# A four-stage transformer block on one core: weighing TensorE's changes of array layout together with the stages' lag

## The chip, the cores and the metric

The kernel runs on one core of a Trainium2 chip. The metric is the time of one execution on the device in microseconds; the median of several runs is compared. Profiles are of one execution each.

## The reference

The input x holds 16 sequences of 512 positions with 256 features, in float32. Four residual steps follow each other; each begins with a layer norm:

```python
x = x + attn_a(layernorm(x))   # 16 heads of 16; window |i-j| <= 32 and 4 global positions; biases
x = x + ffn(layernorm(x))      # silu(x wg') * (x wu'), 768 wide, then wd'; integer weights / 127
x = x + attn_b(layernorm(x))   # 16 heads; causal; rotary q and k in the numerator,
                               # num = exp(q_rot k_rot' / 4), den = sum over all keys of exp(q k' / 4)
x = x + ffn(layernorm(x))      # the same weights as above
```

In `attn_b` the denominator is summed over all 512 keys with the unrotated q and k, and the causal mask is applied to num / den.

## The kernel before

The four steps are four **stages**, named a, f, b and h. Each stage handles one sequence at a time, as 4 tiles of 128 positions (NT) and 2 halves of the features (NC). Up to four sequences are under way at once, since x has 4 buffers; so at any time the stages work on different sequences.

TensorE's work comes in **pieces** of a few matmuls. Each piece has a layout of the array (`lying`):

- FULL: 128 rows and 128 columns. These are the transposes after the layer norm (`lt_*`, L454), the projections (`psc_*`, L534, and `psv_*`, L512), the output products (`po_*`, L488), stage a's transposes of its weights (`tp`, L772, and `pgp`, L809 and L811) and its small global products (`ya` at L855, `sgp`, `gq`, `vgp`, `tg`, `og`, `yg`).
- ROWS: four strips of 32 rows, used at once, each with the products of one head. These are the scores `sa` of stage a (L663, 4 pieces per sequence), and in stage b the scores for the denominators `dn` (L1102, 16 pieces) and for the numerators `nm` (L1162, 10 pieces). Such a piece takes four of the eight PSUM banks.
- COLS: four strips of 32 columns: weights times values, `ya` of stage a (L842, 8 pieces) and `yb` of stage b (L1222, 10 pieces).

The other engines take the results out of PSUM. For `dn`, ScalarE applies the exponential with a sum to each of the four banks (L1083). For `nm`, ScalarE writes exponentials to `ptb` (L1129, two buffers), GpSimd cuts them to the causal part (L1138), and `yb` uses them. For `tp`, ScalarE and VectorE copy to `pt` (three buffers), and `ya` uses those.

The order of the instructions is written by a planner in Python, the class `Plan`, when the program is built. Every stage is a set of generators (threads) that yield one operation after another, each with an engine, an estimated time, what it needs (names with due times) and the buffers that it takes. `Plan.run` keeps a time for each engine and each buffer. At each step it computes when every thread's next operation could start, looks at the earliest, and gathers the operations of that engine that could start within 0.05 us of it (`soon`). On TensorE it chooses among them by a key; first comes a rank (-2 for the transposes after the layer norm, 0 for most). The planner charges BORDER, 0.2 us (L84), when the layout of a piece differs from that of the one before (`self.lying`).

`progress` (L137) says how far a thread's stage is: the number of its sequence, plus the stage's lead (LEAD, L192), plus the TensorE time that this stage has had for this sequence, divided by the stage's SHARE (L193). The thread that is least far is served first.

The planner's order is kept on all engines and on SP's DMA queue, as the instruction streams are emitted in the order of its choices. So another choice on TensorE also moves the operations that follow from it on the other engines.

## Time and profile before

| | before |
|---|---|
| median of 3 runs | 2706.07 us (2703.79 to 2711.95) |
| the profiled execution, its own time | 2707.05 us |
| its span, first to last instruction | 2705.3 us |
| busy: TensorE, VectorE, ScalarE, GpSimd | 2645.4, 1572.2, 1461.4, 740.3 us |
| mean granted clock of TensorE | 0.992 |

The busy time of TensorE (PE) is the time in which at least one matmul was under way. Weight loads have a row of their own (PEld). A group of instructions is named by its line, engine and operation, with the tile that it writes and those that it reads.

### The profile page before, as it was taken

To read this page: it belongs to the slowest core of one execution; us is meant where nothing else is said; L and a number is where in the kernel's file an instruction comes from. 1 tells how busy PE (TensorE), PEld (TensorE's weight loads), DVE (VectorE), ACT (ScalarE), POOL (GpSimd) and SP (SyncE) were. 2 spreads that over 40 slices of the span, in tenths; PEclk is the share of its full clock that TensorE was granted. 3 is DMA by queue.
4 is the path that set the end of the run, shared out by engine and by line. 5 is a ranking of instruction groups with operands and counts; after the bars stand their busy time and mean duration, and the time that the engine had idled before them with its cause. 6 is when DMAs were issued, how large, how long until landed. Compare 5 with 4: busy or idle time off the path is not lost.

```text
span 2705.3 us, 52423 instructions
## 1 busy us (share of the span) xinstructions
PE 2645.4 (98%) x21700; PEld 1511.9 (56%) x21700; DVE 1572.2 (58%) x3062; ACT 1461.4 (54%) x3553; POOL 740.3 (27%) x916
## 2 busy tenths in 40 slices
PE   6999999999999999999999999999999999999997
PEld 4655556455565655656466564655656456564444
DVE  7865656466565655746466564565745557464422
ACT  2346564755547455474645647455474654646472
POOL 4323324032241313313133231322313133130201
PEclk8999999999999999999999999999999999999999
DMA  4000010000000000010000100000000000100000
GB/s 134 24 23 1 5 35 1 23 17 23 17 2 23 17 23 17 1 38 2 23 17 6 34 2 23 17 23 17 2 23 17 23 17 1 31 2 8 1 9 8
DMA packets 26574, 49.10 MB, mean 18 GB/s; under 512 B 2336, under 2 KB 21216, under 8 KB 26336
## 3 DMA queue, kind: packets, MB, share of 16 engines
q1 hardware_dynamic: 24976, 44.83, 5.7%
q8 instruction: 170, 2.79, 0.4%
q10 hardware_dynamic: 1360, 0.93, 0.2%
q14 instruction: 68, 0.56, 0.1%
HBM read 13.77 MB, written 8.39 MB: 8 GB/s over the span
## 4 chain that ended last, share of the span: by engine, by line
PE 90%; DVE 6%; issue 3%; ACT 1%; POOL 1%; DMA 0%; ACTq 0%; POOLq 0%; DVEq 0%
PE dn L1102 10%; PE nm L1162 6%; PE psc_gh L534 6%; PE psc_uh L534 6%; PE po_h L488 6%; PE po_f L488 6%; PE psc_uf L534 6%; PE psc_gf L534 6%; PE yb L1222 5%; PE tp L772 4%; PE sa L663 2%; PE ya L842 2%; PE psv_a L512 2%; PE po_a L488 2%; PE psv_b L512 2%
## 5 line engine op out<-in xcount | busy, mean ns | idle before, releaser
L1083 ACT ACTIVATE dn<-dn 128x512 f32<-128x512 f32 x1024 | 598.1, 584 | 136.7 <-PE dn L1102 135.5
L1129 ACT ACTIVATE ptb<-nm 128x512 f32<-128x512 f32 x640 | 329.7, 603 | 278.3 <-PE nm L1162 278.2
L708 POOL TENSOR_TENSOR sc<-sc,sm 128x1056 f32<-128x1056 f32 x128 | 247.4, 1952 | 227.7 <-DVE sm L706 220.7
L1102 PE MATMUL dn<-kt,qb 32*128 32x512 f32 x2048 | 291.6, 635 | 0.0
L1138 POOL TENSOR_SCALAR_AFFINE_SELECT ptb<-ptb 128x512 f32<-128x512 f32 x256 | 157.9, 636 | 446.2 <-ACT ptb L1129 437.9
L715 ACT ACTIVATE sc<-sc 128x1056 f32<-128x1056 f32 x128 | 138.5, 1096 | 137.4 <-POOL sc L708 136.0
L693 DVE TENSOR_TENSOR sc<-sa,mask 128x512 f32<-128x512 f32 x256 | 159.8, 682 | 59.4 <-PE sa L663 59.1
L534 PE MATMUL psc_gh<-xnt_h,wg_sb 128*128 128x512 f32 x384 | 189.2, 615 | 3.2 <-DVE vb L523 3.0
L1083 ACT ACTIVATION_READ_ACCUMULATOR dn<-dn 128x1 f32 x1024 | 191.7, 187 | 0.0
L1162 PE MATMUL nm<-qr,kr 32*128 32x512 f32 (+3 forms) x2048 | 191.0, 461 | 0.4 <-ACT ptb L1129 0.3
L717 DVE TENSOR_REDUCE sm<-sc 128x8 f32<-128x1056 f32 x128 | 157.3, 1242 | 55.2 <-ACT sc L715 55.2
L534 PE MATMUL psc_uh<-xnt_h,wu_sb 128*128 128x512 f32 x384 | 186.9, 609 | 0.0
L534 PE MATMUL psc_gf<-xnt_f,wg_sb 128*128 128x512 f32 x384 | 182.9, 599 | 1.6 <-DVE xnt_f L462 1.6
L534 PE MATMUL psc_uf<-xnt_f,wu_sb 128*128 128x512 f32 x384 | 183.2, 599 | 0.0
L488 PE MATMUL po_h<-wd_sb,ht_h 128*128 128x256 f32 x768 | 181.3, 386 | 0.0
L1102 PEld LDWEIGHTS dn<-kt,qb 32*128 32x128 f32 x2048 | 90.0, 183 | 160.0 <-ACT dn L1083 88.1
L488 PE MATMUL po_f<-wd_sb,ht_f 128*128 128x256 f32 x768 | 179.2, 383 | 0.0
L1222 PE MATMUL yb<-ptb,vb 128*32 128x512 f32 (+3 forms) x2048 | 170.1, 441 | 8.4 <-POOL ptb L1138 8.3
L421 POOL TENSOR_SCALAR rstd_f<-mv_f 128x4 f32<-128x4 f32 x16 | 3.7, 232 | 613.8 <-DVE mv_f L417 613.8
L488 PEld LDWEIGHTS po_h<-wd_sb,ht_h 128*128 128x128 f32 x768 | 141.0, 190 | 45.9 <-issue 13.3
L706 DVE TENSOR_REDUCE sm<-sc 128x8 f32<-128x1056 f32 x128 | 156.3, 1237 | 0.0
L488 PEld LDWEIGHTS po_f<-wd_sb,ht_f 128*128 128x128 f32 x768 | 141.3, 190 | 26.5 <-issue 3.3
(168 smaller groups left out, 4201.3 us busy)
## 6 DMA issues: line engine op xcount, KB each, us to landing
vw<-va SPq DMA_DIRECT2D x32, 576.0 KB, 5.8
x<-in_x_dram SPq DMA_DIRECT2D x16, 512.0 KB, 3.9
out_dram<-x SPq DMA_DIRECT2D x16, 512.0 KB, 2.9
vw<-va SPq DMA_DIRECT2D x32, 144.0 KB, 5.0
raw_wg_sb<-in_w_gate_dram SPq DMA_DIRECT2D x1, 768.0 KB, 8.8
raw_wu_sb<-in_w_up_dram SPq DMA_DIRECT2D x1, 768.0 KB, 10.2
raw_wd_sb<-in_w_down_dram SPq DMA_DIRECT2D x1, 768.0 KB, 10.9
wqkv_sb<-in_wqkv_dram SPq DMA_DIRECT2D x1, 768.0 KB, 11.7
```

The source lines that it names most:

```text
L488: nc.tensor.matmul(po[:, :D], y_of(c), w_sb[:, c, :], start=(c == 0), stop=(c == n - 1))
L534: nc.tensor.matmul(ps, w_sb[:, kc, lo : lo + P], x_in[:, kc, :], start=(kc == 0), stop=(kc == NC - 1))
L693: nc.vector.tensor_tensor(flat[:, 4 * j : 4 * j + 4, 0:P], ps[j].rearrange("p c two w -> p (c two) w"), mask.unsqueeze(1).to_broadcast([P, ...
L706: nc.vector.tensor_reduce(small[:, 0, hs], part, AX.X, ALU.max, negate=True)
L708: nc.gpsimd.tensor_tensor(part, part, small[:, 0, hs].unsqueeze(2).to_broadcast([P, H // 2, P + NG]), ALU.add,)
L717: nc.vector.tensor_reduce(small[:, 1, hs], part, AX.X, ALU.add)
L1083: nc.scalar.activation(ps[j], ps[j], AF.Exp, scale=SCALE, accum_out=den[:, t, h : h + 1])
L1102: nc.tensor.matmul(ps[j], tiles["qb"][rows, par, oc, t * P : (t + 1) * P], tiles["kt"][rows, oc, :], start=True, stop=True,)
L1129: nc.scalar.activation(pt[:, j, :], ps[j], AF.Exp, scale=SCALE)
L1138: nc.gpsimd.affine_select(out=pt[:, :, at : at + P], in_=pt[:, :, at : at + P], pattern=[[0, 4], [1, P]], compare_op=ALU.is_ge, fill=0.0, ...
L1162: nc.tensor.matmul(ps[j][:, at : at + n], tiles["kr"][rows, oc, c * P : (c + 1) * P], tiles["qr"][rows, par, oc, c * P :], start=True, sto ...
L1222: nc.tensor.matmul(y_ps[rows, c * P :], vb[:, c, 4 * oc + j, par : par + 2, :], pt[:, j, at : at + n], start=len(seen) == 1, stop=len(seen ...
```

## The change

The key by which TensorE's next piece is chosen changes. Before, it had three parts: the rank; then, only if TensorE lies in strips, whether the piece lies otherwise (all changes alike); then the progress. Now it has two: the rank, and the progress plus a price for the change of layout, `turn`, in units of sequences. Staying costs 0. Leaving full products costs 0.15, going from rows to columns or back 1.0, and going from strips to full products 5.0. The leads of the stages f, b and h change also: 1.0, 2.0 and 3.0 become 1.069, 1.854 and 2.806. The rest of the diff is blank lines.

```diff
+    def turn(self, lying):
+
+        if lying == self.lying:
+            return 0.0
+        return TURN["out"] if self.lying == FULL else TURN["in"] if lying == FULL else TURN["mid"]
...
                     key=lambda c: (
                         c[1][4],
-                        self.lying != FULL and c[1][1].lying != self.lying,
-                        self.progress(c[1]),
+                        self.progress(c[1]) + self.turn(c[1][1].lying),
                     ),
...
-LEAD = {"a": 0.0, "f": 1.0, "b": 2.0, "h": 3.0}
+TURN = {"out": 0.15, "mid": 1.0, "in": 5.0}
+LEAD = {"a": 0.0, "f": 1.069, "b": 1.854, "h": 2.806}
 SHARE = {"a": 44.0, "f": 33.0, "b": 66.0, "h": 33.0}
```

## The prediction

> **What bounds the kernel now.** I read the head of the page first, then section 5, then the times by stretch, and last the TensorE instructions in order of time.

> ```profile
> span 2705.3 us, 52423 instructions
> PE 2645.4 (98%) x21700; PEld 1511.9 (56%) x21700; DVE 1572.2 (58%) x3062; ACT 1461.4 (54%) x3553; POOL 740.3 (27%) x916
> ```

> TensorE is busy for 98% of the span and no other engine exceeds 58%. The busy times of six stretches (columns: the stretch, then busy time and instructions of PE, PEld, DVE, ACT, POOL, then TensorE's clock and DMA):

> ```profile
> 0.00:620.00 620.00, 585.66 (x5337) 345.55 (x5338) 397.96 (x761) 312.16 (x726) 195.68 (x244) 0.98 0.10 29
> 620.00:2350.00 1730.00, 1730.00 (x14201) 989.40 (x14200) 1030.00 (x2024) 970.38 (x2386) 475.19 (x583) 1.00 0.06 17
> 2625.00:2706.00 81.00, 62.57 (x386) 32.85 (x384) 17.94 (x37) 25.77 (x50) 12.13 (x19) 0.95 0.04 14
> ```

> From 620 to 2350 us TensorE is busy in every microsecond, and the waits of that stretch name none of TensorE's. The last output product of stage h ends there every 163.6 us, sequence after sequence. So no wait is to be saved in the middle: it changes only if TensorE's own stream gets shorter. The matmuls are the same before and after. What can differ is what lies between them, and that is seen in order of time (columns: start, us until the group's last end, engine, line, names, shape, count; the useful number is the difference of two starts):

> ```profile
> 1210.73 1.98 PE L534 MATMUL psc_gf<-xnt_f,wg_sb 128*128 128x512 f32 x4
> 1212.56 1.88 PE L534 MATMUL psc_uf<-xnt_f,wu_sb 128*128 128x512 f32 x4
> 1214.27 1.88 PE L534 MATMUL psc_gf<-xnt_f,wg_sb 128*128 128x512 f32 x4
> ...
> 1316.59 2.00 PE L1102 MATMUL dn<-kt,qb 32*128 32x512 f32 x16
> 1318.52 1.13 PE L512 MATMUL psv_a<-wv_sb,xnt_a 128*128 128x256 f32 x4
> ...
> 1343.01 1.14 PE L1102 MATMUL dn<-kt,qb 32*128 32x512 f32 x8
> 1344.08 1.98 PE L534 MATMUL psc_uh<-xnt_h,wu_sb 128*128 128x512 f32 x4
> 1346.00 1.14 PE L1102 MATMUL dn<-kt,qb 32*128 32x512 f32 x8
> 1347.07 1.98 PE L534 MATMUL psc_gh<-xnt_h,wg_sb 128*128 128x512 f32 x4
> ```

> A full product between full products takes 1.71 us (1212.56 to 1214.27). Just after row strips it takes 1.83; between row strips on both sides, 1.92 (1344.08 to 1346.00). One dn piece between full products takes 1.07 (1343.01), two in a row 1.93 (1316.59), so the second costs 0.86 and the lone one carries 0.21 extra. Pairing neighbouring pieces over the whole trace gives medians for what entering and leaving add: full products 0.104 and 0.094 us (0.055 to enter where it is a transpose), rows 0.104 and 0.109, columns 0.025 and 0.115. So full to rows costs 0.198, rows to full 0.213, full to columns 0.119, columns to full 0.219, rows to columns 0.134, columns to rows 0.219.

> Counting the changes: 356, 331, 130, 155, 87 and 62 in that order, 1121 in all. At those prices they cost 216 us, 8% of the span; 740 of them, 143 us, lie in 620 to 2350. The end has real idleness instead:

> ```profile
> 2656.83 1.23 PE L1222 MATMUL yb<-ptb,vb 128*32 128x256 f32 x16 [1.94 <-POOL ptb L1138]
> 2666.86 2.20 PE L454 MATMUL lt_h<-ident,xn_h 128*128 128x128 f32 x8 [4.63 <-DVE xn_h L426]
> ```

> From 2625.19 (the last product of h's sequence 14 is out) to 2666.86, stage b of sequence 15 runs alone, and the brackets of this stretch sum to 13.3 us of 41.7, 32% idle.

> [...]

> **The change part by part.** It adds no instruction, DMA, buffer or semaphore by itself; it reorders pieces, and with them the work that follows on ACT, DVE, POOL and SP's queue. No engine but TensorE is over 60% in the middle stretch (DVE 1030 of 1730), so their own cost is nothing while TensorE is behind; without that cover, it would show as brackets like those of the end.

> Step 1, **from strips to the other strips before full products** (1.0 against 5.0; before, both ranked alike). I compared each end of a strip visit in 620 to 2350 with when the pieces run later became ready: columns from the end of their copies on ACT and DVE or of POOL's select, rows from four free banks and their buffers. Of 233 changes from rows to full, a column piece was ready in 32; of 97 from columns to full, a row piece in 10. The other 288 were forced, and the new rule has nothing else to take there.

> Step 2, **full products keep TensorE unless strips are 0.15 behind**. Against stage a's full products b's strips stand as before (0.15 against a lead lowered by 0.146). Stage a's own strips (sa, ya) do change: they no longer win a tie with a's full products and wait for b's next visit. There are 325 visits in 620 to 2350, on average 3.8 us apart; 44 consist of one column piece (33 ya, 11 yb). Attached to a row visit, such a piece saves 0.119 + 0.219 + 0.213 - (0.134 + 0.219) = 0.198 us. The 32 of step 1 are mostly these same pieces. So 44 x 0.198 = 8.7, and the 10 of step 1 another 10 x 0.198 = 2.0: 10.7 us, and over the whole span by changes (1121/740) **16 us**. Bounds: 0, if the pieces still go singly; above, the second rival.

> Step 3, **gathering**. 41 visits are a single nm and 126 a single dn. The dn's I leave: their four exponentials and accumulator reads take 4 x (0.584 + 0.187) = 3.08 us on ACT, and the dn's start 2.99 us apart (1343.01, 1346.00): ACT and the banks set their beat, not the choice. If one nm in four meets another row piece, 10 visits go at 0.198 + 0.213: 4.1 us, over the span **6 us**. Nearest row for the lower bound: none meets, 0.

> Step 4, **the leads**. In the middle they shift phases, which TensorE's full stream hides. In the drain, h comes 0.194 x 163.6 = 32 us earlier, b 24 us earlier, f 11 us later. Between h's sequence 14 and b's 15 this moves 0.048 x 163.6 = 7.9 us of cover away, at 32% idle **2.5 us** lost. Bounds: -5 (b's last chain starts sooner) and +21 (all of h's 32 us uncovered, 10 us, and f's 11 us straight on the end).

> Sum: -16 - 6 + 2.5 = -20 us. The profiled execution took 2707.05 us (span 2705.3), 1.0 above the median of 2706.07; 2707 - 20 = 2687, against the median **2686 us**.

> **The rivals.** *Strips gather strongly.* If full products are held long enough that a quarter of the visits join others, 81 x 0.411 = 33 us in the middle, 50 over the span: 2656 us. For it: visits average only 3.8 us apart, and 211 of 325 hold one piece. Against: 126 of those follow ACT's beat.

> *The order hardly changes what counts.* With 288 of 330 ends forced, and a shift of phases that makes as many single visits as it removes, 3 us are left: 2703 us. The same would show if the lowered lead of b cancelled the 0.15 everywhere.

> *The drain gets longer: slower.* Place: from h14's last product to h15's transposes. Stage b's chain (nm, exponentials, select, yb) doesn't depend on the choice and needs filling work; h14 goes earlier and f15 later, so filling is spent before b15 needs it. Price up to +21 us. It decides once it exceeds what the changes save: with 8 saved instead of 22, the result is 2706 + 21 - 8 = 2719 us. For it: 32% idle there already. Against: b is brought forward too.

> **How the numbers follow.** Forecast 0.53 (2670 to 2698), strong gathering 0.16, no difference 0.13, slower 0.18. A measurement can tell about 0.3%, 8 us, so "same" is 2698 to 2714. Faster is 0.53 + 0.16 = 0.69. The range runs from a little beyond 2656 down to 2648 and up to 2722, past the slower rival; about one in ten lies outside on each side at most.

> **What would show it.** Steps 1 and 2: changes between full products, rows and columns fall from 1121 to about 1010, single ya visits nearly vanish, rows-to-columns and columns-to-rows changes grow above 87 and 62; the prices of each change stay. Step 3: longer nm groups, dn still single at 3 us. Step 4: brackets before yb, dbp and lt_h in the last 100 us sum to 13 to 18 us. The period in the middle falls from 163.6 to about 162.3 us, with no waits of TensorE there. The forecast is wrong if changes don't fall, if TensorE gets waits in the middle, or if the drain loses over 10 us.

## The result, and the profile after

The changed kernel takes 2746.81 us (median of 5 runs, 2745.42 to 2748.78), the kernel before 2706.65 us (5 runs). The ratio is 1.015, with a 95% interval of 1.0137 to 1.0164: slower by 40 us, outside the predicted range. The span of the profiled execution is 2747.0 us, 41.7 us longer.

The head of the page after:

```profile
span 2747.0 us, 52475 instructions
PE 2664.6 (97%) x21700; PEld 1539.5 (56%) x21700; DVE 1556.0 (57%) x3062; ACT 1471.8 (54%) x3553; POOL 739.6 (27%) x916
```

TensorE executes the same 21700 matmuls and stays the bound. But the stretch that had no waits now has some. The waits of TensorE from 620 to 2350 us (engine and piece, who ended the wait; total us, times, longest) and the busy times there (PE, PEld, DVE, ACT, POOL, then clock and DMA):

```profile
PE ya L840 <- DVE pt L775: 26.2, 11, 2.4
```

```profile
620.00:2350.00 1730.00, 1703.80 (x13823) 984.99 (x13827) 1001.30 (x1983) 942.08 (x2273) 471.51 (x578) 0.98 0.06 16
```

It is one wait of 2.38 us in each sequence of this stretch, always the same: `ya`, in the middle of a piece, for a copy to `pt` on VectorE (L775; it was L777 before). All of TensorE's waiting there is this line, 1730.00 - 1703.80 = 26.2 us. Here is one such place, TensorE in order of time (start, us, engine, line, names; in brackets the idle time before):

```profile
984.41 0.66 PE L770 MATMUL tp<-ident,sc 128*128 128x128 f32 x4
984.90 1.96 PE L532 MATMUL psc_qa<-xnt_a,wq_sb 128*128 128x512 f32 x4
986.79 0.43 PE L840 MATMUL ya<-pt,vw 128*32 128x64 f32 x16
989.61 0.56 PE L840 MATMUL ya<-pt,vw 128*32 128x64 f32 x16 [2.38 <-DVE pt L775]
990.10 2.09 PE L1100 MATMUL dn<-kt,qb 32*128 32x512 f32 x8
992.12 1.22 PE L853 MATMUL ya<-pgs,vg 64*128 64x128 f32 x4
993.27 3.62 PE L532 MATMUL psc_uh<-xnt_h,wu_sb 128*128 128x512 f32 x4
```

In the kernel before, the two halves of such a piece (32 matmuls) run as one group:

```profile
1283.84 0.65 PE L842 MATMUL ya<-pt,vw 128*32 128x64 f32 x32
```

In the listing of the changed kernel, look at the lines after the wait, too. The dn piece takes 2.0 us (990.10 to 992.12) where 1.07 is usual, and the up product 3.45 us (993.27 to 996.72) where 1.72 is. The busy times by stretch give the reason (the third column from the end is TensorE's clock):

```profile
974.60:989.60 15.00, 12.62 (x92) 7.00 (x90) 14.69 (x29) 5.85 (x15) 4.92 (x5) 1.00 0.01 2
989.60:996.60 7.00, 6.99 (x32) 3.27 (x33) 1.17 (x3) 2.49 (x8) 0.00 (x0) 0.51 0.00 0
```

After each wait TensorE runs at half clock for 6.83 us, which costs 3.4 us more. And the first of these lines shows VectorE, from which the copy comes, busy for 14.69 of the 15 us up to the end of the wait.

**Where the 41.7 us are.** I counted the changes of layout (1001 instead of 1121) with the prediction's prices, TensorE's idle time before its matmuls, and the stretches at half clock, of which half is lost:

| us | before | after | difference |
|---|---|---|---|
| changes of layout | 215.6 | 192.4 | -23.2 |
| idle time of TensorE | 55.5 | 78.0 | +22.5 |
| lost to half clock (half of 41.8 and 126.3) | 20.9 | 63.2 | +42.3 |
| the rest of the span | 2413.3 | 2413.4 | +0.1 |
| span | 2705.3 | 2747.0 | +41.7 |

The rest is the same within 0.1 us, so for the span as a whole these three terms are enough. The change did save what it was to save; waits took it back, and the clock took nearly twice as much again. By place: stage h's sequence 0 ends 14.9 us earlier, the next twelve sequences (called the middle below) take 44.9 us longer (167.2 us each instead of 163.6), the rest of the span 11.8 us longer. Place by place the three terms leave several microseconds open, because work moves from one stretch to another and because the profile's busy time hides some short waits (dn pairs that take 2.95 us instead of 1.93, below).

### The profile page after: what moved, and what is told of

Its sections match the earlier page's. It is cut to its first block, busy times and chain, and to the rows that moved or that the text cites. A ratio compares the mean times of both kernels' runs of the same rounds, so it can differ in the third digit from the quotient of the medians.

```text
span 2747.0 us, 52475 instructions
## 1 busy us (share of the span) xinstructions
PE 2664.6 (97%) x21700; PEld 1539.5 (56%) x21700; DVE 1556.0 (57%) x3062; ACT 1471.8 (54%) x3553; POOL 739.6 (27%) x916
## 4 chain that ended last, share of the span: by engine, by line
PE 91%; DVE 5%; ACT 2%; POOL 1%; issue 1%; DMA 0%; ACTq 0%; POOLq 0%; DVEq 0%
PE dn L1100 10%; PE psc_uh L532 7%; PE po_h L486 6%; PE nm L1160 6%; PE psc_gh L532 6%; PE po_f L486 6%; PE psc_uf L532 6%; PE psc_gf L532 6%; PE yb L1220 5%; PE tp L770 4%; PE sa L661 2%; PE ya L840 2%; PE psv_a L510 2%; PE psc_ka L532 2%; PE po_a L486 2%; PE po_b L486 2%
## 5 line engine op out<-in xcount | busy, mean ns | idle before, releaser
L1100 PE MATMUL dn<-kt,qb 32*128 32x512 f32 x2048 | 297.4, 657 | 0.0
L532 PE MATMUL psc_uh<-xnt_h,wu_sb 128*128 128x512 f32 x384 | 205.6, 662 | 0.0
L1100 PEld LDWEIGHTS dn<-kt,qb 32*128 32x128 f32 x2048 | 96.2, 189 | 113.5 <-issue 57.6
L492 DVE TENSOR_TENSOR x<-x,po_h 128x256 f32<-128x256 f32 x64 | 27.0, 422 | 217.4 <-PE po_h L486 217.4
```

Source lines behind the costliest of these rows:

```text
L532: nc.tensor.matmul(ps, w_sb[:, kc, lo : lo + P], x_in[:, kc, :], start=(kc == 0), stop=(kc == NC - 1))
L1100: nc.tensor.matmul(ps[j], tiles["qb"][rows, par, oc, t * P : (t + 1) * P], tiles["kt"][rows, oc, :], start=True, stop=True,)
```

## The experiments

The line numbers of the experiments' kernels differ by a few from those above.

**1. The two halves of the change, and the wait alone.** First theory: the leads moved stage b's rotary work on VectorE onto the copy that ya needs; the new key is innocent. `e1_turn_only`:

```diff
-LEAD = {"a": 0.0, "f": 1.069, "b": 1.854, "h": 2.806}
+LEAD = {"a": 0.0, "f": 1.0, "b": 2.0, "h": 3.0}
```

> The new key with the old leads (1, 2, 3). My theory of the 40 us: in every sequence one ya piece is issued 2.4 us before its pt is copied, because VectorE's queue is late there behind stage b's rotary work, and the wait is followed by 6.8 us at half clock (3.4 us lost); the lower lead of b moved b's rotary work onto ya, so it is a matter of the leads' phase. By it this kernel has no wait of 2.4 us per sequence, about 1000 changes of layout, and takes about 2685 us. Rival: the new key itself, which holds ya back and then takes it in a hurry, makes the wait; then the wait of about 2.4 us and the half clock are here too and the time is about 2745 us. Second rival: the lost time is in the drain, from the leads; then about 2690 us without any waits in the middle in either part.

Measured: 2793.31 us, ratio 1.0321 (1.0304 to 1.0338), with 965 changes. `e2_lead_only` has the old key and the new leads:

```diff
-                        self.progress(c[1]) + self.turn(c[1][1].lying),
+                        self.lying != FULL and c[1][1].lying != self.lying,
+                        self.progress(c[1]),
```

> The new leads (1.069, 1.854, 2.806) with the old key. Theory (phase from the leads): the wait before ya and the half clock are here, with about 1120 changes: 2706 + 12 x 5.8 = about 2775 us. Rival (the key makes the wait): no such wait in the middle, 2706 to 2718 us. Second rival (drain): no wait in the middle, and the drain 12 us or more longer: 2718 us or above.

Measured: 2783.92 us, ratio 1.028 (1.0265 to 1.0295), with 1150 changes. Neither half has the wait of 2.38 us, and each is slower than the whole. TensorE's waits from 560 to 2300 us in the first and in the second (the longest lines):

```profile
PE nm L1160 <- DVE sc L691: 13.3, 6, 2.2
PE lt_h L452 <- DVE xn_h L424: 9.4, 15, 0.9
PE dbp L1189 <- POOL rdcb L539: 6.2, 6, 1.0
```

```profile
PE psv_b L511 <- DVE x L493: 9.6, 5, 1.9
PE psc_qb L533 <- DVE xnt_b L461: 5.1, 4, 1.3
PE dn L1101 <- DVE th_h L965: 2.9, 4, 0.7
```

My theory in that form fell: the wait belongs to neither half but to the order that both make together, and each half alone makes an order with other waits, most of them for VectorE again. That the second comes near the 2775 us of the theory is luck, since its waits are others. In the first kernel, waits also hide in what the profile counts as busy: 15 of its dn pairs ahead of po_h take 2.95 us instead of 1.93 (8 in the kernel before), about 7 us more. The rest of its span is 2463.5 us by the same sum, 50 more than before; in the second it is 2434.4, 21 more. Most of that stays open.

`e3_pt_late` takes only the premature choice of ya away:

```diff
+LATE = 3.0
...
-                    how = dict(gives=(("u", op.k["u"]),), makes=f"pt_{me}.{t}.{n}")
-                    go(one(dve(S, op.end, **how) if par else act(S, op.end, **how), keep), -1)
...
+                        op = yield (dve(S, at, **how) if par else act(S, at, **how))
+                        plan.at[name] = op.end + (LATE if par else 0.0)
...
+                    go(late(op), -1)
```

> The changed kernel, but the planner counts the VectorE copies to pt as 3 us later than it did, for ya's sake alone; no instruction is added. Theory: ya is no longer issued before its pt is there, so the 12 waits of 2.38 us and the 12 half-clock stretches (3.4 us each) go: 2747 - 12 x 5.8 = about 2677 us, with about 1000 changes. Rival (the half clock has another cause than the wait): only the waits go, 2747 - 29 = 2718 us. Rival (the loss is in leads and drain): 2735 us or above.

Measured: 2759.36 us, ratio 1.0191 (1.0176 to 1.0206). The theory and the first rival missed. The number lies where the second rival put it (2735 us or above), but its cause, leads and drain, is not shown: the waits of ya are gone from 620 to 2350 us and half clock falls there from 75.1 to 6.8 us, and yet the order is a new one, with 1053 changes and waits in other places of that stretch:

```profile
PE psc_gh L533 <- DVE xnt_h L461: 10.6, 5, 2.1
PE psv_b L511 <- DVE th_h L971: 8.7, 6, 1.5
```

So a changed order can't serve to price a wait: it brings its own. The next experiments leave TensorE's order as it is.

**2. What a wait costs.** `e4_stall_long` is the kernel before with a wait put in by hand, once per sequence:

```diff
+        if stall:
+            nc.tensor.matmul(ps[:, 0:P], tok[:, 0:P], tok[:, 0:P], start=True, stop=True)
+            for _ in range(REPEAT):
+                nc.gpsimd.tensor_tensor(tok, tok, tok, ALU.mult)
+            nc.tensor.matmul(ps[:, 0:P], tok[:, 0:P], tok[:, 0:P], start=True, stop=True)
...
+                channels(op, xnt[me], wu_sb, f * P, f"u{me}_{f}", stage == "h" and f == 4),
```

> The kernel before, its order untouched, with one wait put into TensorE's stream in every sequence: ahead of the fifth up product of stage h a small matmul reads a tile, GpSimd rewrites that tile four times (256 columns each, about 0.65 us), and a second small matmul needs it: a wait of about 2.9 us. Theory (a wait of this length also halves the clock for 6.8 us): 16 x (2.9 + 0.2 + 3.4) = 104 us more, about 2810 us, with a half-clock stretch in each sequence. Rival (the wait costs only itself): 16 x 3.1 = 50 us more, about 2756 us.

Measured: 2784.94 us, ratio 1.0292 (1.0277 to 1.0308), between the theory and its rival. The wait and the stretches around it:

```profile
1207.91 0.70 PE L542 MATMUL psc_uh<-tok 128*128 128x128 f32 x2 [2.83 <-POOL tok L541]
1208.40 3.40 PE L544 MATMUL psc_uh<-xnt_h,wu_sb 128*128 128x512 f32 x4
```

```profile
1204.60:1208.00 3.40, 0.57 (x7) 0.38 (x3) 0.35 (x1) 2.49 (x8) 2.45 (x4) 1.00 0.00 0
1208.00:1211.40 3.40, 3.40 (x6) 1.41 (x6) 0.00 (x0) 0.00 (x0) 0.00 (x0) 0.51 0.00 0
1211.40:1214.80 3.40, 3.40 (x17) 1.08 (x16) 0.69 (x1) 1.91 (x7) 0.00 (x0) 0.99 0.01 2
```

The period grows from 163.6 to as much as 168.8 us for a wait of 2.82: the clock is lost as well, but for a stretch of 3.41 us and not of 6.83, and in 14 sequences of 16. `e5_stall_short` is the same with one repetition.

> The same as the long wait, but GpSimd rewrites the tile once: a wait of about 0.9 us. Theory: a short wait leaves the clock alone, 16 x (0.9 + 0.2) = 18 us more, about 2724 us. Rival (any wait halves the clock): 16 x (1.1 + 3.4) = 72 us more, about 2778 us. Rival (a wait is made good elsewhere, since TensorE is not the bound in truth): 2707 us for both lengths.

Measured: 2729.51 us, ratio 1.0089 (1.0074 to 1.0104); the wait is 0.75 us, the clock never falls in the middle, and the period grows by 1.5 us (the two small matmuls are in it). So a wait of 0.75 us costs only itself, and one of 2.82 us costs the clock too in most sequences. Both rivals fall.

**3. Why the copy is late.** VectorE in the changed kernel, ahead of the late copy:

```profile
975.84 0.99 DVE L1012 TENSOR_TENSOR tmpb<-tmpb,sins 128x512 f32<-128x512 f32 x1
976.93 1.57 DVE L1014 TENSOR_TENSOR tmpb<-tmpb 128x512 f32<-128x512 f32 x1
978.54 1.37 DVE L547 TENSOR_SCALAR qr<-tmpb,masks 128x512 f32<-128x512 f32 x1
...
983.81 0.68 DVE L1012 TENSOR_TENSOR tmpb<-tmpb,sins 128x512 f32<-128x512 f32 x1
984.41 0.42 DVE L521 COPY vb<-psv_b 128x256 f32<-128x256 f32 x1
984.74 0.68 DVE L1014 TENSOR_TENSOR tmpb<-tmpb 128x512 f32<-128x512 f32 x1
```

GpSimd in the same stretch:

```profile
974.92 1.36 POOL L1006 TENSOR_TENSOR kr<-kt,cos 128x512 f32<-128x512 f32 x1 [0.45 <-ACT kt L1062]
976.64 1.32 POOL L1006 TENSOR_TENSOR tmpb<-tmpb,cos 128x512 f32<-128x512 f32 x1 [0.35 <-ACT tmpb L1021]
978.36 1.27 POOL L1006 TENSOR_TENSOR kr<-kt,cos 128x512 f32<-128x512 f32 x1 [0.40 <-ACT kt L1062]
```

The operations of L1012 and L1014 take 0.68 us later on, alone, and up to 1.57 us while GpSimd multiplies by the cosines. In this trace the products that end at 976.28 and 977.96 us (974.92 + 1.36 and 976.64 + 1.32) are followed about 0.55 us later by the ends of the two operations beside them (976.83 and 978.50). The trace shows the overlap and the longer times, not by what mechanism. The planner counts no such thing: its estimate of an operation on VectorE is the same whatever GpSimd does. `e6_cos_small` cuts these products short and keeps the order:

```diff
-                nc.gpsimd.tensor_tensor(dst, src, cos, ALU.mult)
+                nc.gpsimd.tensor_tensor(dst[:, 0:8], src[:, 0:8], cos[:, 0:8], ALU.mult)
...
-            nc.vector.tensor_tensor(dst, dst, t1, ALU.add)
+            nc.vector.tensor_tensor(dst, t1, t1, ALU.add)
```

> The changed kernel with the same order of TensorE, but stage b's rotary product with the cosines on GpSimd is cut to 8 of 512 columns, and the addition after it on VectorE takes the sine part twice: the cosine part is left out, VectorE keeps every instruction. Theory: the copy to pt that ya waits for is late because VectorE's operations take up to twice as long while GpSimd's large products run (0.69 us becomes 1.57 us), 2.3 us in all before that copy. So the wait of 2.38 us and the half clock go: 12 x 5.8 = 69 us less, about 2678 us. Rival (VectorE is late for its own sake, the planner's durations are too short): the wait stays within 0.5 us of 2.38, about 2745 us.

Measured: 2660.28 us, ratio 0.9833 to the kernel before (0.9817 to 0.985). The longest of VectorE's operations at L1012 is now 694 ns (1431 before the edit), and from the first shuffle to the copy 11.7 us pass instead of 13.8. No wait of TensorE is left between 620 and 2300 us, and the period is 161.3 us. The gain of 87 us is more than the 69 that I expected, in part because the start gains too: h's sequence 0 ends at 365.2 us instead of 378.1. The rival, that the planner's durations of VectorE are too short in themselves, falls. `e7_split_act` computes all of it and relieves VectorE in another way:

```diff
-                split_heads(tiles["qb"], qt, oc, par)
+                nc.scalar.activation(
+                    tiles["qb"][:, par, oc, :], qt, AF.Copy, scale=par_mask[:, par : par + 1]
+                )
```

> The changed kernel with the same order of TensorE; the four splits of q into even and odd heads (qb) per sequence go from VectorE to ScalarE, which is idle for two thirds of that stretch. Everything is computed. Theory: about 1.9 us or more is taken from VectorE's queue ahead of the late copy, the wait falls from 2.38 us to 0.5 or less and the clock stays up: about 2680 us. Rival: ScalarE's exponentials are pushed back and dn waits instead: 2740 us or more.

Measured: 2664.98 us, ratio 0.9852 (0.9837 to 0.9867). The place of the wait:

```profile
955.59 1.88 PE L532 MATMUL psc_qa<-xnt_a,wq_sb 128*128 128x512 f32 x4
957.40 0.91 PE L840 MATMUL ya<-pt,vw 128*32 128x64 f32 x32
958.24 1.14 PE L1102 MATMUL dn<-kt,qb 32*128 32x512 f32 x8
959.31 0.71 PE L853 MATMUL ya<-pgs,vg 64*128 64x128 f32 x4
```

The two halves of ya are one group again, no wait is seen from 560 to 2300 us, and the period is 161.6 us. This version beats both kernels, and takes 82 us less than the changed kernel. VectorE's operations still take up to 1.73 us beside GpSimd's here; it is VectorE's lateness that goes, and the wait goes with it.

**4. The controls.** The same two edits on the kernel before, `e8_before_cos_small` and `e9_before_split_act`, tell whether they help any order.

> The kernel before with the cosine product on GpSimd cut to 8 columns and the addition taking the sine part twice (the cosine part is left out): the control to the same edit in the changed kernel (2660 us). Theory: no wait in the middle to take away, 2700 to 2706 us. Rival (less work on GpSimd helps any order): about 2665 us.

> The kernel before with the four qb splits per sequence on ScalarE instead of VectorE, order and results as before: the control to the changed kernel with that edit (2665 us). Theory: before has no wait of TensorE between 620 and 2350 us, so there is nothing to take away: 2700 to 2708 us, and the 40 us between the two are what the new order brings once its wait is gone. Rival (moving the splits helps any order): about 2665 us here too.

Measured: 2694.77 us, ratio 0.9957 (0.9942 to 0.9972), and 2698.33 us, ratio 0.9972 (0.9961 to 0.9983). Both gain a little more than I expected, nearly all of it in the first and the last stretch; the period stays 163.6 us. Between the second control and the changed order with the same edit lie 2698.3 - 2665.0 = 33 us: what the new order is worth without its wait. By the sum above the spans differ by 35.3 us: 23.2 are changes of layout, 11.3 idle time, all of it outside the middle, and 1.3 half clock; the rest is 0.5 us longer. The prediction had the first of these, but not the idle time, of which 8.3 us lie before the end of h's sequence 0.

The same edit on the two halves, `e10_turn_split` and `e11_lead_split`:

> The new key with the old leads, and the qb splits on ScalarE. Without the splits moved it took 2793 us, with waits of nm (up to 2.2 us), lt_h and others on VectorE. Theory (its loss, too, is VectorE being late beside GpSimd's rotary products): most of these waits go and it comes to 2665 to 2700 us. Rival (other lateness, in stages that the rotary work doesn't touch): above 2760 us.

> The new leads with the old key, and the qb splits on ScalarE. Without the splits moved it took 2784 us, with waits of psv_b (1.9 us), psc_qb and lt_h on VectorE. Theory: part of the waits goes, and with about 1150 changes of layout it cannot come below the kernel before: 2706 to 2760 us. Rival (the leads alone bring the gain): below 2690 us.

Measured: 2768.44 us, ratio 1.0231 (1.0214 to 1.0248), and 2724.69 us, ratio 1.0068 (1.0053 to 1.0083). With the new key alone, the wait of nm remains as it was (13.3 us in 6 waits), so its loss is mostly of another kind: the rival holds (above 2760 us), and the theory falls. With the leads alone, 59 us of 78 go, and what is left is above the kernel before, as expected.

**5. Where the wait stands.** Why 6.8 us at half clock in the changed kernel and 3.4 in the fourth experiment? `e12_stall_in_ya` puts a wait between the halves of a ya piece of the kernel before:

```diff
+                    if t == NT - 1 and n == 3:
+                        for m in range(2):
+                            nc.tensor.matmul(
+                                y_ps[0:32, 0, 0:U],
+                                tok[:, 0:32],
+                                tok[:, 0:U],
+                                start=False,
+                                stop=False,
+                                skip_group_check=True,
+                            )
+                            for _ in range(0 if m else REPEAT):
+                                nc.gpsimd.tensor_tensor(tok, tok, tok, ALU.mult)
```

> The kernel before, its order untouched, with a wait of about 2.2 us put between the two halves of the last second ya piece of each sequence, which is where the changed kernel waits (a small column matmul reads a tile of zeros, GpSimd rewrites it three times, a second one needs it; zeros are added to the result). It asks why the long wait ahead of a full product halved the clock for 3.4 us while the changed kernel's wait of 2.38 us halved it for 6.8 us. If what lies around the wait decides (column and row strips): 6.8 us at half clock, 16 x (2.2 + 0.3 + 3.4) = 94 us more, about 2800 us. If it doesn't: 3.4 us at half clock, 16 x (2.2 + 0.3 + 1.7) = 67 us more, about 2773 us. If a wait of 2.2 us is under the limit in this place: 40 us more, about 2746 us.

Measured: 2760.36 us, ratio 1.0198 (1.0181 to 1.0215). The waits are 2.13 to 2.57 us; only five of the twelve from 450 to 2420 us are followed by half clock, each for 3.41 us. None of the three expectations holds. After which idle times the clock fell is told in the last section. Why it stays down for a second stretch of 3.41 us in the changed kernel stays open, for the places are less alike than the expectation says. In the changed kernel a dn piece of row strips (2.0 us at half clock) comes right after the ya piece that waits. Here full products fill the stretch at half clock, from 982.80 to 986.21 us:

```profile
982.75 2.06 PE L490 MATMUL po_a<-wo_sb,yt 128*128 128x256 f32 x4
984.61 1.82 PE L456 MATMUL lt_b<-ident,xn_b 128*128 128x128 f32 x8
```

So the experiment does not test whether strips after the wait keep the clock down. The other traces do not settle it: in `e1_turn_only` one stretch at half clock holds 2.0 us of row strips and ends after 3.41 us (at 2656.1 us), while those with more than 2.7 us of them last 6.83.

## Why the prediction was wrong, point by point

- **What bounds the kernel** held: TensorE's stream, and the price of each change. In the changed kernel a dn between full products takes 1.071 us, and an up product between rows 1.914 us, as before. One reading was too strong: busy in every microsecond does not mean that nothing waits. In the middle, six dn pairs ahead of po_h take 2.95 us instead of 1.93, as here in the chain of work that ended last:

```profile
860.04 2.95 PE dn L1102 x16
```

In the changed kernel no pair of the middle does so: about 6 us that the prediction did not see.

- **Steps 1 to 3** held in size: 1001 changes instead of the forecast 1010, 192.4 us instead of 215.6, so -23.2 against the forecast -22. In 620 to 2350 us, visits that are a single ya fell from 33 to 10. Step 3 was wrong on dn: single dn visits, which it left as they were, fell from 126 to 81, and single nm visits by 21, from 41 to 20, not by 10. So that the sum came out within 2 us is partly luck. (Step 1 counts 233 + 97 = 330 ends of strip visits; the changes of that stretch are 231 + 94 = 325, as many as the visits. Nothing hangs on it.)
- **Step 4**, the drain, was 2.5 us by forecast. In the last stretch (from the end of h's sequence 12) idle time falls from 21.1 to 16.6 us and the loss to half clock rises from 7.2 to 11.9: zero together. The brackets of the last 100 us sum to 11.0 us instead of 13.3. But here, too, busy time hides waits. After the last product of h's sequence 14, five dn pieces of b's sequence 15 stand alone:

```profile
2653.11 9.99 PE L1100 MATMUL dn<-kt,qb 32*128 32x512 f32 x39
2662.23 1.22 PE L1160 MATMUL nm<-qr,kr 32*128 32x512 f32 x1
```

They take 9.1 us (2653.11 to 2662.23). Five in a row need 1.07 + 4 x 0.86 = 4.5, and half clock from 2658.88 us on adds 1.7: about 3 us are hidden waits. So the slower rival has its place and its mechanism, filling work that ends too early, but at about 3 us and not 21; it is right in sign for another reason. The last stretch is 11.8 us longer in all. Most of that, as I read it, is work moved there, since h is further ahead by the 14.9 us that it gains at the start; that is not shown.

- **The step that failed** is the sentence ahead of the steps: that the cost to the other engines "is nothing while TensorE is behind", and in step 4, that phases are hidden by TensorE's full stream. I took the cover from an average (VectorE busy 1030 us of 1730). The order is fixed ahead by the planner's estimates, so one late result stops everything that stands behind it in TensorE's order, here for 2.38 us in each sequence. In the 15 us up to the end of the wait, VectorE was busy for 14.69. The term that was put at nothing measured +28.1 us of waits in the middle.
- **The second term left out** is the clock, +41.0 us in the middle. The prediction had no case in which a wait costs more than itself. The trace of the kernel before showed it: its wait of 3.01 us at 2452.8 us is followed by a gate product of 3.78 us, where 1.71 is usual, in the chain of work that ended last.
- **That it would show**: "the forecast is wrong if ... TensorE gets waits in the middle" was the right sign to look for; the case was named and given no price.

That the kernel before has no visible wait in its middle looked like slack. It is a property of that one order: four other orders (the change, its two halves, the late pt) each have waits of their own there.

## What to carry to other kernels

Where a planner fixes the order of all engines ahead, count what a reorder saves and then ask of every engine that feeds the bound one, in short windows and not by its average, whether it has room where the new order needs it. Waits of two to three microseconds that recur are worth removing one by one: here, moving four small operations per sequence turned a loss of 40 us into a gain of 41, of which 33 remain against the old order with the same edit. Test a suspected wait with an edit that keeps the order, and with the same edit on the old kernel as control.

## What the runs showed of the hardware that I had not expected

**VectorE beside GpSimd.** In the changed kernel's trace an addition of 128x512 took 0.68 us alone (984.74 us) and 1.57 us beside GpSimd's product (976.93 us). Ahead of the late copy, three operations in a row were lengthened, by 0.31, 0.89 and 0.89 us: together the 2.1 us by which the stretch from the first shuffle to the copy is longer than in `e6_cos_small`. With these products cut to 8 columns, and the cosine part left out, the changed kernel takes 2660 us instead of 2747, of which the control gains 11 us as well.
